# A two-layer decoder on one core: the first groups of two stages of layer 0 prepared inside the stage before, and first attention's steps reordered

## The chip, the core and the metric

The kernel runs on one core of a Trainium2 chip. The metric is the device time of one execution in microseconds (us). The kernel before was run three times: 3530.05 us median, 3529.0 to 3537.34. A core has five engines that work side by side, each with its own queue of instructions: PE (matrix multiplication and transposes, with weight loads as a second track), DVE (vector), ACT (activation), POOL (GpSimd), and SP, which here issues DMAs. An engine works off its queue in order; it waits where an operand, or the memory for its result, isn't ready.

## The reference

The input x is [32, 100, 256] in fp32: 32 sequences of 100 positions. The context is [32, 361, 192]. Cut to what matters here:

```
x = x + attention(layernorm(x))                 # layer 0: causal, 16 heads of 16
x = x + cross_attention(ctx, layernorm(x))      # keys and values from layernorm(ctx) and from
                                                # layernorm(x); q and k rms-normed; 4 heads of 64
x = x + dense_layer(layernorm(x))               # see below
# layer 1: attention, cross attention, routed experts, likewise added to x

def cross_attention(ctx, latents):
    xn, ln = layernorm(ctx) * g + b, layernorm(latents) * g + b
    q  = ln @ Wq.T
    kv = concat([xn @ Wkv.T, ln @ Wlkv.T])      # 361 + 100 keys
    ...

def dense_layer(x):
    q_in = rope(x)                              # queries and keys from rope(x), values from x
    a  = causal_attention(q_in @ Wq.T + bq, q_in @ Wk.T + bk, x @ Wv.T + bv)
    x1 = layernorm(x + a @ Wo.T + bo)
    gates = softmax(x1 @ Wg.T + bg)             # the best 2 of 8 experts, by their gates
    return layernorm(x1 + sum(gate_e * (x1 @ We_e.T + be_e)))
```

## The kernel before

**Stages.** Layer 0 has three: first attention (from about 8 to 290 us of the profile), cross attention (290 to 774) and the dense layer, attention with rope followed by the experts (774 to 1300). Layer 1 follows with three stages that the change leaves alone. x stays on the chip, as eight tiles `xs[g]`, one for each group of G = 4 sequences (NG = 8 groups, B = 32 sequences).

**What sets the order.** Each stage's body stands in an `in_order()` block: PE, DVE, ACT and POOL get their instructions in the order in which the code calls them. DMAs on SP are placed by a scheduler. PSUM is shared by all stages: two double tiles for scores (`sc_tile`) and four banks for everything else (`mm_tile`), handed out in rotation as they come free.

**Both attentions of layer 0** are made by one function, `heads_attention` (L275). `norm(g, part)` makes the normed rows of a group in four parts; `turn(g)` returns them transposed; `queries_or_keys(g, m)` makes one of four pieces of the group's queries and keys. Its loop (from L461) has one step for each sequence s. With i = s % 4, a step issues, in this order: the scores of s+1 (L356) and their mask's first half; for i = 0 the transposes of the next group, for i = 1 piece 1, for i = 2 pieces 2 and 3; for i = 1 and 3 a part of the next norm; division of the sums of s-1 (`divided`: four transposes L418, reciprocal L423, product L425); `lowered` (maximum on DVE, L376, subtraction on POOL, L377) of the first half and the second mask; `turn_weights(s)` (16 transposes L389, copies of eT on ACT, L394); for i = 0 piece 0; for i = 2 `norm(g + 1, 1)`; then the second `lowered`, the values, the transposes of o (L431), the exponentials (L382) and the output. A caller's `fill(s, part)` is called at four places of a step. First attention calls it with an empty `fill`. There `norm` does two things: part 1 is the statistics (four BATCH_NORM_STATS2, four aggregates and two small operations), part 2 the centring (L183). Its transposed rows are copied out of PSUM one half by DVE (L131) and one by ACT (L133).

**Cross attention** starts with a prologue: contexts 0 and 1 loaded, both of context 0's parts of the norm, the latent statistics and centring of group 0 (`latents`, parts 0, 1 and 2), the first part of context 1's, and the transposed latents. Its loop runs from n = -4 to B, and each step works on several sequences at once: contexts are loaded six ahead, normed five ahead, transposed four ahead, keys and values made three ahead. The latents' own keys, values and queries (`own_keys_values`, tile x_wl in the profile's names) come in each step behind the output of the sequence before. `keys_turned` transposes keys and queries and copies them to kT (ACT, L724) and qT (DVE, L732), two buffers each.

**The dense layer** has its `norm` at L934: part 0 the statistics, part 1 the scaled rows xl (four activations on ACT, L192), part 2 eight transposes (L949) with two copies to xlT on ACT (L952), part 3 the rope on DVE (L960 to L965: xrT). In `heads_attention` all four parts run for group 0 before the first scores, and for group 1 after the first exponentials. The expert weights (f0_we, 2 MB) and their bias are loaded at the end of first attention, with the stage's other weights; the first matmul that reads them stands at 887.5 us.

Of the kernel before, what the change touches and what calls it, by code (L numbers as in the profile page):

```python
# [18 lines left out]
P = 128  # L19
B, T, D = 32, 100, 256  # L20
S2, DC = 361, 192
G = 4
# [4 lines left out]
E = 8  # L27
# [39 lines left out]
def kernel(ctx: ExitStack, tc: tile.TileContext, io: dict, out: bass.AP):  # L67
# [207 lines left out]
    def heads_attention(pool, w, wo, bias, norm, turn, res, fill):  # L275
# [171 lines left out]
        with in_order():  # L447
            for part in range(4):
                norm(0, part)
# [9 lines left out]
            for part in range(4):  # L459
                norm(1, part)  # L460
            for s in range(B + 1 + fill.steps):  # L461
                g, i = s // G + 1, s % G
                more = s + 1 < B
                if more:
                    ps = scores(s + 1)
                    masked(s + 1, 0, ps[0])
                if g < NG:
                    if i == 0:
                        turned_[g] = turn(g)
                    for m in ((), (1,), (2, 3), ())[i]:  # L470
                        queries_or_keys(g, m)
                if i in (1, 3) and g + 1 < NG:
                    norm(g + 1, i - 1)
                fill(s, 0)
                if 1 <= s <= B:
                    divided(s - 1)
                if more:
                    lowered(s + 1, 0)
                    masked(s + 1, 1, ps[1])
                if s < B:  # L480
                    turn_weights(s)
                fill(s, 1)
                if i == 0 and g < NG:
                    queries_or_keys(g, 0)
                if i == 2 and g + 1 < NG:
                    norm(g + 1, 1)
                if more:
                    lowered(s + 1, 1)
                    values(s + 1)
                if 1 <= s <= B:  # L490
                    turn_sums(s - 1)
                if more:
                    exponentials(s + 1, 0)
                if s < B:
                    sums(s)
                fill(s, 2)
                if 1 <= s <= B:
                    output(s - 1)
                if more:
                    exponentials(s + 1, 1)  # L500
                if i == 3 and g + 1 < NG:
                    norm(g + 1, 3)
                fill(s, 3)
# [11 lines left out]
    x0_wo = weight(w1, "x0_wo", D, D)  # L515
    with tc.tile_pool(name="a0", bufs=2) as pool:
# [19 lines left out]
        def fill(s, part):  # L536
            pass
# [11 lines left out]
    f0_we = weight(w2, "f0_we", D, E * D)  # L549
    f0_eb = plain(w2, "f0_eb", [E, D])  # L550
    rope = plain(w2, "rope", [P, 3, T])
    kch = CCH + [(S2, T)]
    NK = S2 + T
    with tc.tile_pool(name="x0", bufs=2) as pool, tc.tile_pool(name="x0p", bufs=1) as fixed:


        cbuf, kbuf, mbuf = [], [], []
        for n in range(2):
            cb = fixed.tile([P, 3, DC], F32, tag=f"cb{n}", name=f"cb{n}")
            nc.gpsimd.memset(cb[96:128, 2, :], 0.0)  # L560
            cbuf.append(cb)
            mb = fixed.tile([T, NK], F32, tag=f"mb{n}", name=f"mb{n}")
            nc.gpsimd.memset(mb[:, S2:], 0.0)
            mbuf.append(mb)
# [9 lines left out]
        def latents(g, part):  # L574
            if part < 2:
                lns[g] = stats(xs[g], G, twice=True, tag="l", half=part, got=lns.get(g))
            else:
                ln = pool.tile([T, G, D], F32, tag="ln", name="ln", bufs=1)
                centered(ln, xs[g], G, lns[g])
                lns[g] = ln  # L580

        def latents_turned(ln):
            lnT = pool.tile([P, 2, GT], F32, tag="lnT", name="lnT")
            transposed(lnT, ln, "x0_lg", "x0_lb", tiles=mm_tile)
            return lnT

        cbs, cns, cTs, kbs, kns, vbs, kTs, exs, eTs, oTs = {}, {}, {}, {}, {}, {}, {}, {}, {}, {}

        def context(b):
            cb = cbuf[b % 2]  # L590
            nc.sync.dma_start(
                cb[:, 0:2, :], io["ctx"][b, 0:256].rearrange("(c p) d -> p c d", p=P)
            )
            nc.sync.dma_start(cb[:105, 2, :], io["ctx"][b, 256:S2])
            cbs[b] = cb

        def context_normed(b, part):
            if part == 0:
                cns[b] = stats(cbs[b], 3, P, tag="c")
            else:  # L600
                cn = pool.tile([P, 3, DC], F32, tag="cn", name="cn")
                centered(cn, cbs.pop(b), 3, cns[b], P)
                cns[b] = cn

        def context_turned(b, c):

            if c == 0:
                cTs[b] = pool.tile([P, 2, S2], F32, tag="cT", name="cT")
            cn, cT = cns[b], cTs[b]
            pt = mm_tile()  # L610
            for k, (k0, kn) in enumerate(CCH):
                if c == 0:
                    nc.tensor.transpose(pt[:, k0 : k0 + kn], cn[:kn, k, 0:P], ident[:kn, :kn])
                    continue
                for e in range(2):
                    nc.tensor.matmul(
                        pt[64 * e : 64 * e + 64, k0 : k0 + kn], cn[:kn, k, P:DC],
                        ident[:kn, :kn], start=True, stop=True, tile_position=(0, 64 * e),
                    )
            gain, bias = col("x0_xg", c), col("x0_xb", c)  # L620
            if c == 0:
                return lambda: nc.scalar.activation(
                    cT[:, 0, :], pt[:, :S2], AF.Identity, bias=bias, scale=gain
                )
            cns.pop(b)
            return lambda: nc.vector.tensor_scalar(
                cT[:, 1, :], pt[:, :S2], gain, bias, ALU.mult, ALU.add
            )
# [54 lines left out]
        def squares(b):  # L683
            sq = pool.tile([P, 5, D], F32, tag="sq", name="sq", bufs=1)
# [26 lines left out]
        def keys_turned(b, c):  # L711
            if c == 0:
                kTs[b] = [
                    pool.tile([P, 2, NK], F32, tag="kT", name="kT"),
                    pool.tile([P, 2, T], F32, tag="qT", name="qT"),
# [121 lines left out]
        lns, lnTs = {}, {}  # L837

# [4 lines left out]
        with in_order():  # L843
            for b in range(2):
                context(b)
            context_normed(0, 0)
            latents(0, 0)
            context_normed(0, 1)
            latents(0, 1)
            latents(0, 2)  # L850
            context_normed(1, 0)
            lnTs[0] = latents_turned(lns.pop(0))


            for n in range(-4, B + 1):
# [6 lines left out]
                at(n - 1, output)  # L862
                at(n + 2, roots)
# [26 lines left out]
                at(n + 1, divided, 0)  # L890

# [37 lines left out]
    with tc.tile_pool(name="f0", bufs=2) as pool:  # L929
        xls = {}  # L930

        xrTs, xlTs = {}, {}

        def norm(g, part):  # L934


            if part == 0:
                xls[g] = stats(xs[g], G, tag="n", shift=True)
            elif part == 1:
                xl = pool.tile([T, G, D], F32, tag="xl", name="xl", bufs=3)  # L940
                scaled(xl, xs[g], G, xls[g])
                xls[g] = xl
            elif part == 2:
                xl2 = xls[g].rearrange("p g (d two) -> p g d two", two=2)
                xlT = xlTs[g] = pool.tile([P, 2, GT], F32, tag="xlT", name="xlT")
                for c in range(2):
                    ps = mm_tile()
                    for i in range(G):
                        nc.tensor.transpose(  # L949
                            ps[:, i * T : (i + 1) * T], xl2[:, i, :, c], ident[:T, :T]  # L950
                        )
                    nc.scalar.copy(xlT[:, c, :], ps[:, :GT])  # L952
            if part == 3:
                xlT = xlTs[g]
                xrT = xrTs[g] = pool.tile([P, 2, GT], F32, tag="xrT", name="xrT")
                xwT = pool.tile([P, 2, GT], F32, tag="xwT", name="xwT", bufs=1)
                l4, r4, w4 = (
                    x.rearrange("p c (i t) -> p c i t", t=T) for x in (xlT, xrT, xwT)
                )
                nc.vector.tensor_tensor(r4, l4, bc(bc(rope[:, 0], 1, G), 1, 2), ALU.mult)  # L960
                for c in range(2):
                    nc.vector.tensor_tensor(
                        w4[:, c], l4[:, 1 - c], bc(rope[:, 1 + c], 1, G), ALU.mult
                    )
                nc.vector.tensor_tensor(xrT, xrT, xwT, ALU.add)  # L965
# [98 lines left out]
        def gated(n):  # L1064
            if n < E * NG:

                tag = "xg" if n < 2 * (B - 2 * G) else ("xg", "xlT", "xrT")[(n // 2 + 1) % 3]
                xg = pool.tile([P, 2, GT], F32, tag=tag, name="xg")
# [83 lines left out]
        def gates():  # L1152
# [7 lines left out]
            pool, f0_w, f0_wo, ("f0_bq", "f0_bk", "f0_bv"), norm, turn_group, res, fill  # L1160
        )

# [1149 lines left out]
```

## Time and profile before

One execution was profiled. It took 3532.22 us; its span from the first to the last instruction is 3530.5 us. The mean granted clock of PE was 0.977 of full speed.

| stretch, us | length | PE busy | DVE busy | ACT busy | POOL busy | granted clock |
|---|---|---|---|---|---|---|
| start, 0 to 8 | 8 | 0.00 | 0.23 | 1.28 | 1.03 | 1.00 |
| first attention, 8 to 290 | 282 | 254.62 | 197.96 | 162.36 | 112.48 | 0.95 |
| cross attention, 290 to 774 | 484 | 466.80 | 338.91 | 289.11 | 366.58 | 0.98 |
| dense layer, 774 to 1300 | 526 | 479.19 | 365.84 | 231.56 | 208.18 | 0.97 |
| layer 1, 1300 to the end | 2230.5 | 2146.92 | 966.24 | 919.20 | 555.17 | 0.98 |

A line of a timeline has the start, the busy time of the group, the engine, the line of the code, the operation, the tiles written and read by their names in the program, the shapes, the count, and in square brackets the idle time before it with the instruction that ended it. A wait in brackets on PE is time in which PE did nothing. The granted clock is a mean over the stretch that is asked for.

### The profile page before, as it was taken

The page shows a single profiled execution, that of the slowest core. Times are in us where ns is not written, and L with a number is a line of the kernel's source. Part 1 is how long each engine was busy: PE and PEld are TensorE (multiplying, and loading weights), DVE is VectorE, ACT ScalarE, POOL GpSimd, SP SyncE. Part 2 cuts the span into 40 slices and gives each one's busy share as a digit, 9 for nine tenths or more (in the row PEclk, how much of TensorE's full clock was granted, in tenths as well). Part 3 has the DMA queues.
Part 4 walks back from the last instruction along what each step waited for, and adds up shares of the span by engine and source line. Part 5 has one row for each costly group of instructions (what it writes and reads, how often), then busy time and mean ns, then how long its engine had stood idle before and what let it go on. Part 6 is the DMA issues. An engine that isn't in the chain of part 4 may idle for free. (4 is left out here: it accounts for less than half of the span.)

```text
span 3530.5 us, 66384 instructions
## 1 busy us (share of the span) xinstructions
PE 3347.5 (95%) x25978; PEld 2258.8 (64%) x25978; DVE 1869.2 (53%) x5328; ACT 1603.5 (45%) x3533; POOL 1243.4 (35%) x917
## 2 busy tenths in 40 slices
PE   7998999988999978999899999999999989999997
PEld 5675666656666643333566666666666658899997
DVE  5777777747777646655455465564645542011111
ACT  4664666656544315567454454544444442211111
POOL 3445887854434330001223333333333332012221
PEclk9999999999999989999999999999999999999999
DMA  2001100000111111000100000000000003456665
GB/s 84 2 2 61 26 23 23 20 18 9 29 29 27 36 47 26 1 1 1 46 10 19 21 24 20 26 21 19 24 23 19 24 24 109 143 168 192 181 181 146
DMA packets 109218, 168.15 MB, mean 48 GB/s; under 512 B 14996, under 2 KB 89628, under 8 KB 108444
## 3 DMA queue, kind: packets, MB, share of 16 engines
q1 hardware_dynamic: 94238, 145.60, 13.7%
q0 software_dynamic: 12688, 15.36, 2.4%
q8 instruction: 207, 3.39, 0.4%
q10 hardware_dynamic: 1982, 2.95, 0.2%
q14 instruction: 103, 0.84, 0.1%
HBM read 138.32 MB, written 28.82 MB: 47 GB/s over the span
## 5 line engine op out<-in xcount | busy, mean ns | idle before, releaser
L1704 POOL TENSOR_TENSOR ex<-ex,rc 100x1444 f32<-100x1444 f32 x128 | 332.0, 2594 | 785.2 <-DVE rc L1703 743.5
L1695 ACT ACTIVATE ex<-s,nmx 100x361 f32<-100x361 f32 x512 | 303.2, 594 | 143.6 <-DVE nmx L1686 143.6
L377 POOL TENSOR_TENSOR s<-s,nmx 100x800 f32<-100x800 f32 x128 | 195.0, 1523 | 338.9 <-DVE nmx L376 220.9
L1302 ACT ACTIVATE h<-sc,cols 128x800 f32<-128x800 f32 x256 | 222.4, 924 | 134.4 <-PE sc L1296 134.0
L1686 DVE CUSTOM_DVE_ANT_0 s<-sc,mb 100x361 f32<-100x361 f32 x512 | 250.3, 526 | 7.7 <-PE sc L1679 7.7
L2159 POOL DMA_INDIRECT acc_dram<-y,xg x57 | 89.0, 1562 | 451.1 <-DVE y L2158 242.8
L2141 ACT ACTIVATE hgT<-sc 128x1024 f32<-128x1024 f32 x57 | 58.4, 1024 | 351.2 <-PE sc L223 351.2
L223 PE MATMUL sc<-xgT,w1b 128*128 128x128 f32 x1824 | 213.1, 275 | 0.4 <-DMA w1b<-in_f_w 0.4
L2158 DVE TENSOR_SCALAR y<-mm,gx 128x256 f32<-128x256 f32 x57 | 27.6, 484 | 348.2 <-PE mm L223 348.2
L223 PEld LDWEIGHTS sc<-xgT,w1b 128*128 128x128 f32 x1824 | 208.2, 192 | 0.7 <-issue 0.6
L223 PE MATMUL mm<-wx,hgT 128*128 x912 | 206.1, 379 | 0.0
L1081 PE MATMUL mm<-xg,f_we 128*128 128x400 f32 x512 | 191.4, 517 | 14.2 <-DVE xg L1069 13.7
L1679 PE MATMUL sc<-kT,qT 64*100 64x361 f32 x1024 | 197.6, 463 | 0.0
L1651 PE MATMUL mm<-x_wa,cT 128*128 128x512 f32 (+1 forms) x512 | 191.1, 496 | 0.1
L1711 PE MATMUL mm<-ident,ex 100*128 100x100 f32 (+1 forms) x1536 | 169.0, 258 | 18.7 <-ACT kT L1633 9.7
L223 PEld LDWEIGHTS mm<-wx,hgT 128*128 128x128 f32 x912 | 169.0, 190 | 20.6
L1729 PEld LDWEIGHTS mm<-eT,vb 128*64 128x64 f32 (+1 forms) x3072 | 136.8, 137 | 67.3 <-issue 66.4
L1621 PE MATMUL mm<-cT,x_wa 128*128 128x361 f32 x512 | 178.3, 471 | 0.7 <-DVE lnT L148 0.7
L1711 PEld LDWEIGHTS mm<-ident,ex 100*128 100x128 f32 (+1 forms) x1536 | 143.6, 152 | 39.8 <-ACT kT L1633 13.9
L174 POOL TENSOR_TENSOR rs<-va,neghalf 100x4 f32<-100x4 f32 (+1 forms) x96 | 95.5, 997 | 206.2 <-DVE va L170 112.7
L1718 ACT COPY eT<-mm 128x400 f32<-128x400 f32 (+1 forms) x256 | 125.7, 491 | 90.0 <-PE mm L1711 88.5
L1729 PE MATMUL mm<-eT,vb 128*64 128x100 f32 (+1 forms) x3072 | 162.2, 254 | 0.0
(346 smaller groups left out, 7220.2 us busy)
## 6 DMA issues: line engine op xcount, KB each, us to landing
w1b<-in_f_w SPq DMA_DIRECT2D x57, 1024.0 KB
wb<-wt_dram SPq DMA_DIRECT2D x64, 200.0 KB
wx<-in_f_w SPq DMA_DIRECT2D x8, 1024.0 KB
xg<-sorted_dram SPq DMA_DIRECT2D x57, 132.5 KB
cb<-in_ctx SPq DMA_DIRECT2D x32, 192.0 KB
cT<-in_ctxT SPq DMA_DIRECT2D x32, 180.5 KB
cT<-in_ctxT SPq DMA_DIRECT2D x64, 90.2 KB
x<-in_x SPq DMA_DIRECT2D x8, 400.0 KB
```

Of the source, the lines that this page charges most:

```text
L223: nc.tensor.matmul(ps, lhsT[k], rhs[k], start=(k == 0), stop=(k == n - 1))
L377: nc.gpsimd.tensor_tensor(sm, sm, bc(nmx, 2, T), ALU.add)
L1081: nc.tensor.matmul(ps[:, :GT], f0_we[:, k, e * D + m * P : e * D + (m + 1) * P], xgs[E * g + e][:, k, :], start=(i > 0 and e == 2 * i and ...
L1302: nc.scalar.activation(h1, both[r2][:, :, :GT], AF.Tanh, bias=col("a1_b1", o))
L1621: nc.tensor.matmul(kTs[u][c][:, :S2], x1_wa[:, m * P : (m + 1) * P], cT[:, 0, :], start=True, stop=False,)
L1651: nc.tensor.matmul(ps[e][:kn, :n], cT[:, 0, at], x1_wa[:, 1024 + c0 : 1024 + c0 + n], start=True, stop=False,)
L1679: nc.tensor.matmul(ps[:T, e, :S2], qT[p0 : p0 + 64, m, tok], kT[p0 : p0 + 64, c, :], start=True, stop=True,)
L1686: nc.vector.tensor_tensor_reduce(s[:, e, :], ps[:T, e, :S2], mb, 1.0, 3.4e38, ALU.add, ALU.min, nmx[:, e : e + 1],)
L1695: nc.scalar.activation(ex[:, 2 * c + e, :], s[:, e, :], AF.Exp, bias=nmx[:, e : e + 1], scale=-1.0, accum_out=sm[:, 2 * c + e : 2 * c + e ...
L1704: nc.gpsimd.tensor_tensor(ex, ex, bc(rc, 2, S2), ALU.mult)
L1711: nc.tensor.transpose(pt[:kn, j * T : (j + 1) * T], ex[:, j, k0 : k0 + kn], ident[:T, :T])
L1729: nc.tensor.matmul(po[64 * e : 64 * e + 64, m * T : (m + 1) * T], vb[k][:kn, v0 + 64 * h : v0 + 64 * h + 64] if k < 2 else vb[2 + u % 2][: ...
```

## The change

First attention (the calls with bias None): the statistics of the next group move from behind `turn_weights` in the step with i = 2 to ahead of `divided`; the next group's rows are turned at the end of the step with i = 3, no longer after the scores of the next step; piece 0 of queries and keys moves in the step with i = 0 from behind `turn_weights` to right behind the scores.

```diff
     def heads_attention(pool, w, wo, bias, norm, turn, res, fill, ready=0):
...
-                    if i == 0:
+                    if i == 0 and g not in turned_:
                         turned_[g] = turn(g)
-                    for m in ((), (1,), (2, 3), ())[i]:
+                    for m in (((2,), (3,), (), ()) if g == 1 and ready == 2 else ((0,) if bias is None else (), (1,), (2, 3), ()))[i]:
                         queries_or_keys(g, m)
-                if i in (1, 3) and g + 1 < NG:
+                if i >= 1 and (i != 2 or bias is None) and g + 1 < NG:
                     norm(g + 1, i - 1)
...
-                if i == 0 and g < NG:
+                if i == 0 and g < NG and bias is not None and not (g == 1 and ready == 2):
                     queries_or_keys(g, 0)
-                if i == 2 and g + 1 < NG:
+                if i == 2 and bias is not None and g + 1 < NG:
                     norm(g + 1, 1)
...
                 if i == 3 and g + 1 < NG:
                     norm(g + 1, 3)
+                    if bias is None:
+                        turned_[g + 1] = turn(g + 1)
```

Cross attention: the functions of its prologue move ahead of first attention, with their tiles in a pool of their own; the prologue goes, the loop starts one step later, and first attention's `fill` does both:

```diff
         def fill(s, part):
-            pass
+            for f, *args in {
+                (B - 5, 0): ((context, 0), (context, 1)),
+                (B - 3, 0): ((context_normed, 0, 0),),
+                (B - 3, 2): ((latents, 0, 0),),
+                (B - 2, 0): ((latents, 0, 1),),
+                (B - 2, 2): ((context_normed, 0, 1),),
+                (B - 1, 0): ((context_normed, 1, 0),),
+                (B - 1, 1): ((latents, 0, 2),),
+                (B - 1, 3): ((context_normed, 1, 1),),
+            }.get((s, part), ()):
+                f(*args)
+            if s < B:
+                return
+            if part == 0:
+                lnTs[0] = latents_turned(lns.pop(0))
+            elif part < 3:
+                context_turned(0, part - 1)()
+            else:
+                latents(1, 0)
+                context(2)
+                context_normed(2, 0)
...
-            for n in range(-4, B + 1):
+            for n in range(-3, B + 1):
```

To make room, kT and qT have one buffer each instead of two, and the squares of the keys share their tile with a scratch tile of the rope. The expert weights and bias move from the end of first attention to the start of the dense layer, behind layer 1's first weights:

```diff
-    f0_we = weight(w2, "f0_we", D, E * D)
-    f0_eb = plain(w2, "f0_eb", [E, D])
...
-                    pool.tile([P, 2, NK], F32, tag="kT", name="kT"),
-                    pool.tile([P, 2, T], F32, tag="qT", name="qT"),
+                    pool.tile([P, 2, NK], F32, tag="kT", name="kT", bufs=1),
+                    pool.tile([P, 2, T], F32, tag="qT", name="qT", bufs=1),
...
+        f0_we = weight(fixed, "f0_we", D, E * D)
+        f0_eb = plain(fixed, "f0_eb", [E, D])
```

The dense layer: the body of its `norm` becomes `f0_norm(pool, tag, g, part)`, unchanged in what it computes, and is called for groups 0 and 1 in cross attention's last steps:

```diff
+                if n == B - 2:
+                    f0_norm(pool, "sq", 0, 3)
                 at(n + 2, roots)
...
                 at(n + 1, divided, 0)
+                for g_, part in {
+                    B - 8: ((0, 0),), B - 7: ((0, 1),), B - 6: ((1, 0),), B - 5: ((1, 1),),
+                    B - 3: ((0, 2),), B - 2: ((1, 2),), B: ((1, 3),),
+                }.get(n, ()):
+                    f0_norm(pool, "sq", g_, part)
```

`heads_attention` is told so by `ready = 2`: it makes no norm for groups 0 and 1. Group 1 is turned, and its pieces 0 and 1 are made, before the loop; pieces 2 and 3 follow in steps 0 and 1.

```diff
-            for part in range(4):
+            for part in range(4 if ready < 1 else 0):
                 norm(0, part)
...
-            for part in range(4):
+            if ready == 2:
+                turned_[1] = turn(1)
+                for m in range(2):
+                    queries_or_keys(1, m)
+            for part in range(4 if ready < 2 else 0):
                 norm(1, part)
```

## The prediction

> **What bounds the kernel now.** I read the page first, then busy time by stage, then the waits of TensorE (PE), then the timelines of PE, VectorE (DVE) and ScalarE (ACT) at the places that the diff touches.
>
> ```profile
> PE 3347.5 (95%) x25978; PEld 2258.8 (64%) x25978; DVE 1869.2 (53%) x5328; ACT 1603.5 (45%) x3533; POOL 1243.4 (35%) x917
> ```
>
> PE is the bound over all, so only PE's idle time and the time it runs at a lower clock can be won. The table by stage (window, length, busy us of PE, weight loads, DVE, ACT, POOL, granted clock, DMA) says where these are:
>
> ```profile
> 40.00:285.00 245.00, 229.88 (x3011) 173.06 (x3002) 179.54 (x321) 152.36 (x309) 102.59 (x130) 0.97 0.01 2
> 285.00:330.00 45.00, 35.51 (x191) 20.09 (x192) 29.45 (x97) 12.45 (x24) 16.59 (x12) 0.85 0.33 110
> 330.00:745.00 415.00, 414.12 (x3219) 275.23 (x3216) 301.67 (x948) 262.15 (x621) 331.50 (x209) 1.00 0.08 21
> 775.00:830.00 55.00, 41.05 (x413) 29.42 (x414) 30.96 (x60) 30.02 (x57) 15.53 (x20) 0.84 0.09 26
> ```
>
> First attention (40 to 285 us) leaves PE idle for 15 us, the change to cross attention (285 to 330) for 9.5 us at clock 0.85, cross attention itself for nothing, and the start of the dense layer (775 to 830) for 14 us at 0.84. The waits of PE from 40 to 285 us name one releaser (total, times, longest):
>
> ```profile
> PE mm L389 <- ACT ex L382: 12.4, 7, 2.5
> ```
>
> It happens once in each group of four sequences. One such place on PE, with the DVE rows that lead to it, and the clock after it:
>
> ```profile
> 157.76 0.85 PE L389 MATMUL mm<-ident,ex 100*100 100x100 f32 x8
> 160.57 1.29 PE L389 MATMUL mm<-ident,ex 100*100 100x100 f32 x8 [1.95 <-ACT ex L382]
> 161.65 1.92 PE L223 MATMUL mm<-a_w,xT 128*100 128x256 f32 x4
> ```
> ```profile
> 152.17 0.26 DVE L423 RECIPROCAL rc<-mm 100x16 f32<-100x16 f32 x1 [2.26 <-PE mm L418]
> 154.60 0.42 DVE L161 BATCH_NORM_STATS2 st<-x 100x6 f32<-100x256 f32 x1
> 156.93 0.98 DVE L376 TENSOR_REDUCE nmx<-s 100x8 f32<-100x800 f32 x1
> ```
> ```profile
> 162.00:164.00 2.00, 2.00 (x11) 1.22 (x13) 1.97 (x3) 0.84 (x3) 1.52 (x1) 0.50 0.03 8
> ```
>
> The next group's statistics (154.60 to 156.93, 2.33 us) push back the row maximum, so the subtraction on POOL, so the exponential. PE waits 1.95 us and then runs some 3.4 us at half clock (1.92 us for value matmuls that take 1.03 elsewhere). Just before, DVE idles for 2.26 us.
>
> The two changes of stage:
>
> ```profile
> 289.15 1.11 PE L223 MATMUL mm<-a_wo,oT 128*100 128x256 f32 x4 [0.47 <-ACT oT L437]
> 294.56 1.98 PE L210 MATMUL mm<-ident,ln 100*128 100x100 f32 x8 [4.30 <-DVE ln L183]
> 298.47 4.01 PE L223 MATMUL mm<-x_wl,lnT 128*100 128x512 f32 x8
> ```
> ```profile
> 781.08 7.86 PE L223 MATMUL mm<-xrT,f_w 128*128 128x400 f32 x16 [3.60 <-DVE xrT L965]
> 799.06 2.58 PE L949 MATMUL mm<-ident,xl 100*128 100x100 f32 x8 [8.37 <-ACT xl L192]
> 809.12 0.96 PE L356 MATMUL sc<-kT,qT 32*100 32x100 f32 x32
> ```
>
> PE waits 4.30 us for the first normed rows of cross attention, 3.60 us for the rope of group 0 and 8.37 us for the normed rows of group 1 of the dense layer. No arithmetic goes away in this change: what can be won is these gaps and the half clock behind them.
>
> **Part A, first attention's order.** In the third step of a group the statistics move ahead of the reciprocal: they start when the first mask addition ends (149.9) and end at 152.2, inside the 2.26 us idle; reciprocal and o are at most 0.1 us late. The row maximum then starts at 154.7 instead of 156.93, POOL's 1.52 us and ACT's 0.87 us follow, and the exponential ends about 158.2, not 160.5. In the fourth step the second half of the transposes then follows the first without a wait, at full clock. Late next is DVE: x addition, mask (0.98), the centring of the next group's rows (1.76 for four), reciprocal and o end at 160.8. So the o transposes run at 161.0, sums and output to 163.1; the next scores could start at 163.05 instead of 165.92, 2.9 us sooner. Part of this is given back: the eight row transposes (0.91, only moved) stand ahead of these scores, and the q matmuls now stand ahead of the weight transposes and wait for ACT's copy of the turned rows, behind an exponential that is only 0.9 us earlier (end 165.9, copy to 166.4). This is an **added wait** of 0.8 to 1.25 us; behind it on PE stand the transposes of back and of the weights, and ACT's copies wait for those. The scores after come at about 172.0 instead of 173.95: 2.0 us a group. Six groups: **12 us**. Ends: 2 (each new wait brings the half clock, as five of the six old ones did; the group without it is 1.7 us shorter than these) and 18 (the 2.9 is kept).
>
> [...] The row says 0.50 after a gap of 1.95 us. I go by the rows: none for the waits of 0.8 to 1.25 (gaps of 1.05 and 1.29 us elsewhere show no drop), 2 us for the one of 2.5 us in part C. [...]
>
> **Part B, first attention into cross attention.** Context statistics (1.6 us), latent statistics (two of 1.1), centring (0.96 twice, 1.38) and the transposes go into the last four steps of first attention. Steps without a norm there take 5.91 us on PE and have DVE idle 2 to 3 us each; what doesn't fit delays o and back: I count 0.5, 1.3 and 1.2 us in three steps, 3.0 together. Against that, from the last output's end (290.26) to the first latent matmul (298.47), 8.2 us, little stays: lnT at once, its copies, transposes of the context. With the 3.0 included it starts at 294.8, 3.7 sooner; it takes 2.74 as in the steady loop, not 4.01 (1.3); and the 0.5 us of waits in the first context's products go: **5.5 us**. The keys' wait on POOL (2.84 us at 319.91) stays. Ends: 0 (steps delayed twice as much, gaps still at half clock) and 9. On SP's queue contexts 0 and 1 load at step 27, contexts 2 and 3 ahead of the dense layer's weights; that hides the 2.73 us wait for a context at 302.73. The 2 MB of expert weights go to the start of the dense layer, behind layer 1's weights: they took part in the 10 us at 308 GB/s after 290; first use is at 887.5, over 90 us later. Nothing; if the cover were gone, some 7 us.
>
> **Part C, cross attention into the dense layer.** Cross attention's loop has no slack on PE: each of four steps that carry statistics (2.33 on DVE) or scaling (2.07 on ACT) delays the copies of qT or kT that free the banks for the latent matmuls, by about 0.8 us: 3.3 us lost. Transposes, copies and rope of group 0 fall in the waits of the tail (2.60 and 1.29 us at 755 and 759): nothing. From the last output's end (774.35) I count: rope of group 1 on DVE to +3.4, the query bias to +3.75, now behind the rope; PE's four q and k products of 1.34 us to +5.4; ACT's copies to +7.45; scores(0) at +6.9 (before +15.4). Then two q products of group 1, scores(1) at +10.95 (before +27.2). Masks, maxima and exponentials of step 0 end at +14.5 (they took 6.4 us); the copies of group 1's q stand behind these on ACT and hold the banks, so PE waits some 2.5 us, weights to +17.6, and scores(2) comes at +19.75, before at +34.77: 15.0. By scores(4) it is 16.8, as the half clock of 795 to 806 has gone. Less 2 for a new drop, less 3.3: **11.5 us**, ends 5 and 17. One buffer for kT and qT costs nothing: ACT writes kT at 705.6, the scores that read the one before end at 701.3.
>
> **Sum.** 12 + 5.5 + 11.5 = 29 us. Span 3530.5 becomes 3501.5; the profiled execution took 3532.2, 1.7 more; the median of the runs is 3530.05, 2.2 below that. 3501 to 3503: I take 3502.
>
> **Rivals.**
> 1. *The new waits take one part back.* In A the new wait on ACT brings the half clock (A 2 instead of 12), or in C the banks hold PE 8 us longer. For it: five of six gaps. Against it: the new gap is shorter. Time 3512 to 3516.
> 2. *Both.* 29 - 10 - 8, and B at half: about 3523, no change by measure.
> 3. *Slower: one buffer for kT.* If ACT's kT copy had to wait for the scores of the sequence before, each of 31 steps of 14.08 us grows. With 1.5 us a step, 46 - 29: 3548. It decides from 40/31 = 1.3 us a step, which needs scores that end 5.6 us later against the copy than now. Against it: the 4.3 us of slack, and an unchanged order of PE in these steps. A shift of the shared PSUM banks would cost the same way; by the order of instructions 6 of the 64 latent matmul groups wait for ACT after, 3 before, so at most 3 us.
>
> **Chances.** A difference under 0.3% (10.6 us) can't be told from none. Forecast 0.60, rival 1 0.20, rival 2 0.11, rival 3 0.09: faster 0.80, same 0.11, slower 0.09. All parts at their best, 44 us, give 3486; some room below makes 3482; at the top rival 2 is taken in: 3528.
>
> **What would show it.** A: the wait of L389's transposes on the exponential falls from 12.4 to under 3 us, a group from 33.56 to about 31.6, and a new wait on the xT copy appears. B: the gap of 4.30 is gone, last steps a little longer. C: scores(2) about 20 us after the last output, 8.37 gone. Wrong if cross attention's steps exceed 14.08, or if a clock of 0.50 follows the new waits in first attention.

## The result, and the profile after

The changed kernel takes 3512.05 us (median of six runs, 3508.92 to 3513.11), the kernel before on the same chip 3530.19. The ratio is 0.9944, 95% interval 0.9931 to 0.9957: faster by 15 to 24 us, where 29 were forecast. The profiled execution took 3510.88 us, with a span of 3508.4, against 3532.22 and 3530.5 before: 22.1 us by the trace. In the kernel after, line numbers from about 275 on are one or more higher (L389 is L390, L382 is L383).

The waits of PE from 40 to 280 us in the kernel after (total, times, longest):

```profile
PE mm L223 <- ACT xT L133: 5.9, 6, 1.0
PE mm L390 <- DVE qT L312: 3.3, 13, 0.6
PE mm L419 <- ACT back L411: 2.2, 2, 1.5
PE mm L390 <- ACT ex L383: 0.5, 2, 0.3
```

The 12.4 us of waiting for the exponential are down to 0.5. In its place stands, once in each of six groups, the wait for ACT's copy of the turned rows, 1.0 us each. One of them on PE:

```profile
161.91 0.94 PE L223 MATMUL mm<-xT,a_w 128*128 128x400 f32 x2
163.83 0.94 PE L223 MATMUL mm<-xT,a_w 128*128 128x400 f32 x2 [0.98 <-ACT xT L133]
```

Two of the four matmuls of piece 0 run at once, the other two 0.98 us late; the granted clock stays at 1.00. The end of first attention, on PE and, ahead of the second wait, on DVE:

```profile
276.90 0.64 PE L419 MATMUL mm<-ident,back 128*100 128x128 f32 x4 [1.52 <-ACT back L411]
280.70 0.36 PE L432 MATMUL mm<-ident,o 100*128 100x100 f32 x2 [1.23 <-DVE o L426]
288.59 2.74 PE L223 MATMUL mm<-x_wl,lnT 128*100 128x512 f32 x8
```
```profile
275.73 2.27 DVE L183 TENSOR_SCALAR cn<-cb,mv,rs 128x192 f32<-128x192 f32 x3
279.85 0.25 DVE L424 RECIPROCAL rc<-mm 100x16 f32<-100x16 f32 x1
```

The 4.30 us gap is gone and the first latent matmul follows the last output at once (288.59). But the last steps now hold waits of 1.52 us for back and 1.23 us for o; before, the longest of these were 0.53 and 0.90 us. A context's centring and, from 278.25, another context's statistics stand on DVE ahead of the reciprocal that o needs. In cross attention, a step that carries a group's statistics, on PE and on DVE:

```profile
679.81 2.82 PE L223 MATMUL mm<-x_wl,lnT 128*100 128x512 f32 x8 [0.74 <-ACT kT L799]
683.27 1.45 PE L872 MATMUL mm<-ident,ex 100*128 100x100 f32 x14 [0.47 <-POOL ex L863]
```
```profile
680.09 0.16 DVE L173 TENSOR_SCALAR sh<-mv 100x4 f32<-100x4 f32 x1
680.16 0.16 DVE L862 RECIPROCAL rc<-sm 100x2 f32<-100x2 f32 x1
680.24 0.40 DVE L807 TENSOR_SCALAR qT<-mm,gains 128x200 f32<-128x200 f32 x1
```

The second reciprocal and the copy of qT stand behind the statistics. In the steps before it the latent matmuls take the bank that the copy of qT frees, 0.21 us before they start; here they take one that ACT's copy of kT frees, and wait 0.74 us. That copy is not late itself (it starts 14.08 us after the one before); the wait comes from the other bank. Then PE waits 0.47 us for POOL, whose second multiplication needs that reciprocal. The dense layer's start:

```profile
765.83 5.54 PE L223 MATMUL mm<-xrT,f_w 128*128 128x400 f32 x16
781.82 0.55 PE L390 MATMUL mm<-ident,ex 100*100 100x100 f32 x4 [1.84 <-ACT qT L306]
787.24 0.96 PE L357 MATMUL sc<-kT,qT 32*100 32x100 f32 x32
```

The first q products run right behind cross attention's last output, and the waits of 3.60 and 8.37 us are gone; PE waits 1.84 us, and then 0.60, for banks that ACT holds.

The next table goes by the starts of the score matmuls in the timelines (us, profiled executions). "Six groups" is the time from the scores of sequence 4 to those of sequence 28; the next column goes from there to cross attention's first scores. Its first 25 steps take 355.2 to 355.3 us in every kernel and are left out; its last six follow, and then the time to the scores of the dense layer's third sequence, here called the third scores.

| kernel | first scores | six groups of first attention | from there to cross attention's first scores ("the stretch") | last six steps of cross attention | to the third scores of the dense layer | span |
|---|---|---|---|---|---|---|
| before | 22.47 | 201.36 | 72.23 | 75.54 | 48.08 | 3530.5 |
| after | 23.83 | 191.60 | 68.11 | 80.13 | 33.90 | 3508.4 |
| after, again | 24.19 | 191.58 | 68.95 | 80.14 | 34.34 | 3509.1 |
| undo_a | 24.50 | 200.85 | 67.15 | 80.16 | 35.31 | 3520.2 |
| stats_only | 24.23 | 186.03 | 68.62 | 80.14 | 35.45 | 3505.7 |
| xt_dve | 23.89 | 184.12 | 68.95 | 80.10 | 33.86 | 3501.2 |
| undo_b | 23.52 | 195.00 | 62.87 | 80.13 | 35.48 | 3508.1 |
| late_b | 23.06 | 195.09 | 62.73 | 80.13 | 35.17 | 3507.2 |
| we_only | 23.22 | 201.52 | 70.63 | 75.54 | 46.54 | 3528.7 |
| undo_c | 24.28 | 191.57 | 67.11 | 80.73 | 45.05 | 3523.0 |
| so_pq | 24.55 | 186.00 | 67.11 | 75.55 | 30.07 | 3493.0 |
| so_pq_ub | 24.10 | 190.95 | 62.91 | 76.31 | 29.74 | 3495.6 |
| so_pq_hb | 23.22 | 186.06 | 63.56 | 76.45 | 29.76 | 3491.0 |
| best3 | 22.33 | 186.04 | 62.13 | 75.56 | 32.00 | 3490.4 |

### The profile page after: what moved, and what is told of

Its sections match the earlier page's. It is cut to its first block, busy times and chain, and to the rows that moved or that the text cites. A ratio compares the mean times of both kernels' runs of the same rounds, so it can differ in the third digit from the quotient of the medians.

```text
span 3508.4 us, 66389 instructions
## 1 busy us (share of the span) xinstructions
PE 3339.7 (95%) x25978; PEld 2249.4 (64%) x25978; DVE 1872.9 (53%) x5328; ACT 1601.2 (46%) x3533; POOL 1245.6 (36%) x917
```

## The experiments

Times are medians; each has its ratio to the kernel before on the same chip, with its 95% interval. The kernel after has 0.9944 (0.9931 to 0.9957). Most single steps below are smaller than these intervals, so they are read from the traces. Chips differ: before took 3530.19 us on the first and 3532.84 to 3534.94 with the experiments.

**undo_a: first attention's old order, the rest as after.**

```diff
-                if i >= 1 and (i != 2 or bias is None) and g + 1 < NG:
+                if i in (1, 3) and g + 1 < NG:
                     norm(g + 1, i - 1)
...
-                if i == 2 and bias is not None and g + 1 < NG:
+                if i == 2 and g + 1 < NG:
                     norm(g + 1, 1)
...
-                    if bias is None:
-                        turned_[g + 1] = turn(g + 1)
```

(and piece 0 of queries and keys back behind `turn_weights`)

> First attention's order as before, the rest as after. Theory 1 (the old wait on the exponential and the half clock behind it were the cost, part A worth 9.8 us in the trace): six groups back at 33.6 us, the wait of L390 on L383 back at some 12 us, time about 3522. Theory 2 (the half clock falls by chance, so A is worth only the order): at most 2 us slower than after, 3512 to 3514.

3520.24 us, ratio 0.9958 (0.9941 to 0.9975). The six groups are back at 200.85 us and the wait is there again:

```profile
PE mm L390 <- ACT ex L383: 11.7, 6, 2.0
```

Theory 1 holds for the size. What the groups are made of says more. In the kernel before they take 33.75, 33.75, 32.17, 33.68, 33.79 and 34.22 us; in undo_a 33.73, 32.18, 33.69, 33.78, 33.74 and 33.73. One in six is 1.6 us shorter, the third there, the second here. In the kernel before, the wait in that short group is as long as in the others:

```profile
128.39 0.93 PE L389 MATMUL mm<-ident,ex 100*100 100x100 f32 x8 [1.95 <-ACT ex L382]
```

The clock behind it stays at 1.00, and behind the same wait 32 us later it is 0.50. The two differ in where the wait falls. In the traces of before and after, all changes of the granted clock lie 3.413 us or a whole multiple of it apart (50 and 40 stretches of one clock, to within 0.01 us; the half clock behind the second wait lasts from 160.94 to 164.36); the pieces of this length, counted on from there, are called clock windows here. These are the window in which the short group's wait ends, the one behind it, and the one that holds the next group's wait:

```profile
126.81:130.22 3.41, 1.83 (x14) 1.53 (x14) 3.38 (x9) 2.45 (x5) 0.72 (x3) 1.00 0.00 0
130.22:133.63 3.41, 3.41 (x77) 2.59 (x76) 2.56 (x4) 1.85 (x4) 2.94 (x2) 1.00 0.02 5
157.53:160.94 3.41, 1.46 (x16) 1.22 (x14) 3.41 (x8) 1.30 (x3) 2.17 (x4) 1.00 0.00 0
```

The number behind the length is PE's busy time, the last but two is the clock. An edge of the grid, at 126.81, cuts the first wait (126.44 to 128.39), so 1.58 us of idle time are left in its window, and the next window runs at full clock. The second wait lies whole in its window, which leaves 1.95 us, and the next one, from 160.94, runs at half. Of the six such waits in before, the other five leave 1.95 to 2.45 us in one window, and a clock of 0.50 follows each. A group of 33.75 us is 0.38 us shorter than ten windows, so the wait shifts against the grid from group to group: the first three begin 0.41 and 0.01 us behind an edge and 0.37 us ahead of one. By this, which group keeps its clock is a matter of phase.

So the half clock costs some 1.6 us and falls in five groups of six. Against the group without it (32.18), a group of after (31.93) wins only 0.25 us. Most of what part A won is the clock.

**stats_only: of first attention's order, only the statistics move.**

```diff
-                    for m in (((2,), (3,), (), ()) if g == 1 and ready == 2 else ((0,) if bias is None else (), (1,), (2, 3), ()))[i]:
+                    for m in (((2,), (3,), (), ()) if g == 1 and ready == 2 else ((), (1,), (2, 3), ()))[i]:
...
-                    if bias is None:
-                        turned_[g + 1] = turn(g + 1)
```

> Of first attention's order only the statistics are moved; rows are turned and piece 0 of queries is made where they were before. Theory 1 (statistics alone take the wait away; the turning a step sooner only adds the 0.98 us wait on the xT copy and 0.8 us to the step with i = 0): groups of about 31.1 us, some 5 us faster than after, 3507. Theory 2 (the turn has to move as well, or its transposes and piece 0 hold the next step): groups of 32 us or more, 3512 or slower.

3506.73 us, 0.9918 (0.9901 to 0.9935). Groups of 31.0 us, 5.6 less for six than after: theory 1, by the trace; the intervals of the times touch. As it came with the change, turning a step sooner costs 0.94 us a group.

**xt_dve: both halves of the turned rows are copied by DVE.**

```diff
-            transposed(xT, xns.pop(g), tiles=mm_tile)
+            for c in range(2):
+                nc.vector.tensor_copy(xT[:, c, :], ps[c][:, :GT])
```

(from group 2 on, behind the same eight transposes)

> After, but from group 2 on DVE copies both halves of first attention's turned rows out of PSUM, so that no copy stands behind the second exponential on ACT. Theory 1 (the 0.94 us that the turn costs a group is the added wait of piece 0 on ACT's copy): the wait of 0.98 us goes, groups of 31.0 us as with the statistics alone, 5 to 6 us below after. Theory 2 (it is the place of the transposes and of piece 0, ahead of the weights): groups of 31.7 us or more, within 2 us of after.

3504.67 us, 0.9924 (0.9908 to 0.9941). Groups of 30.69 us, and of PE's waits from 40 to 245 us one kind is left:

```profile
PE mm L390 <- DVE qT L312: 3.3, 13, 0.5
```

So theory 1 holds: the cost was the copy on ACT behind the exponential. With the copy on DVE the earlier turn wins 0.3 us a group over stats_only; with it on ACT it loses 0.94.

**undo_b: the prologue back in cross attention's loop.**

```diff
         def fill(s, part):
-            for f, *args in {
...
+            pass
...
+            context_normed(0, 0)
+            latents(0, 0)
...
-            for n in range(-3, B + 1):
+            for n in range(-4, B + 1):
```

> Cross attention's prologue again behind first attention, loop from n = -4, the rest as after. Theory 1 (part B is worth what the trace shows between the last steady step of first attention and the first steady scores, 4.1 to 4.8 us): about 3516.5. Theory 2 (what B wins is lost again in the cross attention it feeds, as its loop is bound elsewhere): within 1 us of after. The start of the kernel tells a third thing: if the first scores are again at 22.5 us instead of 23.8, the early pool has to do with the later start.

3507.5 us, 0.9922 (0.9905 to 0.9938): not slower than after, against theory 1. The span is level with after (3508.1 against 3508.4), as theory 2 had it, but not for its reason: cross attention loses nothing. The trace shows why. The prologue did not go back behind first attention; its instructions stand in the middle of it. DVE and PE in undo_b:

```profile
211.34 0.34 DVE L161 BATCH_NORM_STATS2 st<-cb 128x6 f32<-128x192 f32 x1
...
223.53 0.32 DVE L183 TENSOR_SCALAR ln<-x,mv,rs 100x256 f32<-100x256 f32 x1
223.77 0.42 DVE L426 TENSOR_TENSOR o<-mm,rc 100x256 f32<-100x256 f32 x1
```
```profile
224.33 0.36 PE L432 MATMUL mm<-ident,o 100*128 100x100 f32 x2 [1.93 <-DVE o L426]
```

Context statistics stand there from 211 us on, the context's centring from 217.84 to 219.97, and a piece of the latents' centring right ahead of o, which PE then waits for. The sixth group takes 35.16 us instead of 31.93, but the stretch falls from 68.11 to 62.87 us. Two blocks that are each in a fixed order are still merged by the scheduler. The first scores (23.52 us, after 23.83) do not move with the prologue; the early pool is in this kernel too.

**late_b: as undo_b, and the early tiles are opened behind first attention too.**

```diff
-    ctx_cm = tc.tile_pool(name="x0e", bufs=2, side="right")
...
     close_weights(0)
...
+    ctx_cm = tc.tile_pool(name="x0e", bufs=2, side="right")
```

> After, but with cross attention's prologue and its tiles opened behind first attention as before. Theory 1 (most of B comes from the moved expert weights): that stretch takes 68 to 69 us, as in after (68.1), time within 1 us of after. Theory 2 (B comes from the early prologue): 72 us, 4 us slower than after.

3510.74 us, 0.9934 (0.9917 to 0.995), stretch 62.73, sixth group 35.24: as undo_b, and as neither theory had it. The prologue is merged into first attention wherever the code puts it. In the kernel before, with its tiles in cross attention's pools, it ran at 290 us. That memory of its own is what frees it is an inference; no run changed that alone (the later load of the expert weights, in we_only, does not free it).

**we_only: the kernel before, with the expert weights loaded late.**

```diff
-    f0_we = weight(w2, "f0_we", D, E * D)
-    f0_eb = plain(w2, "f0_eb", [E, D])
...
+        f0_we = weight(fixed, "f0_we", D, E * D)
+        f0_eb = plain(fixed, "f0_eb", [E, D])
```

> The kernel before with one edit: the expert weights and their bias are loaded at the start of the dense layer. Theory 1 (their 2 MB crowded out the contexts at 290 to 300 us, so that moving them is part of what the change wins there): the 2.7 us wait for a context is gone, the stretch from the last steady step of first attention to the first steady scores of cross attention falls from 72.2 us to 68 or 69, time 3 to 4 us below before. Theory 2 (the load was hidden but for a wait that something else takes over, as the prediction had it): within 1 us of before.

3531.05 us, 0.9994 (0.9984 to 1.0003). The stretch falls by 1.6 us, to 70.63, and no wait for a context is left, but PE's wait for the first latent rows (4.30 us before) is the same:

```profile
295.76 1.97 PE L210 MATMUL mm<-ident,ln 100*128 100x100 f32 x8 [4.31 <-DVE ln L183]
```

Both theories miss: the wait of 2.7 us goes, and 1.6 us of it show in the stretch, an amount that the timing alone can't tell from nothing.

**undo_c: the dense layer makes its first norms itself.**

```diff
-                if n == B - 2:
-                    f0_norm(pool, "sq", 0, 3)
...
-                }.get(n, ()):
-                    f0_norm(pool, "sq", g_, part)
...
-            pool, f0_w, f0_wo, ("f0_bq", "f0_bk", "f0_bv"), norm, turn_group, res, fill, 2
+            pool, f0_w, f0_wo, ("f0_bq", "f0_bk", "f0_bv"), norm, turn_group, res, fill
```

> The dense layer makes its own first norms again, the rest as after. Theory 1 (part C is worth 11.1 us by the trace, net of 4.6 lost in cross attention's last steps): about 3523, cross attention's steps at 14.08 to the end, and 14 to 16 us lost between its last output and the third scores. Theory 2 (C is given back later in the dense layer, which waits for something with a fixed date): 3512 to 3516.

3524.3 us, 0.997 (0.9959 to 0.9982), 14.6 us more span than after. Theory 1 for the time; but cross attention's steps are not all back at 14.08. One takes 19.27 us, as group 0's scaling is merged there on ACT, between the copies of keys:

```profile
690.18 1.09 ACT L192 ACTIVATE xl<-x,sh,rs 100x256 f32<-100x256 f32 x2 [2.91 <-POOL sh L176]
691.18 0.35 ACT L734 COPY kb<-mm 105x256 f32<-105x256 f32 x1
691.43 1.09 ACT L192 ACTIVATE xl<-x,sh,rs 100x256 f32<-100x256 f32 x2
```

So this kernel does not quite undo part C either: early norms in a place that nobody chose cost 5.2 us, those of the change 4.6.

**so_pq: three waits taken out.** In first attention only the statistics move (as in stats_only). In cross attention, statistics and scaling of the dense layer's first groups move to steps in which DVE and ACT idle. In the dense layer, the first exponentials move behind the copies of group 1's queries:

```diff
-                    B - 8: ((0, 0),), B - 7: ((0, 1),), B - 6: ((1, 0),), B - 5: ((1, 1),),
                     B - 3: ((0, 2),), B - 2: ((1, 2),), B: ((1, 3),),
...
+                for g_, part in {
+                    B - 6: ((0, 0),), B - 5: ((1, 0), (0, 1)), B - 4: ((1, 1),),
+                }.get(n, ()):
+                    f0_norm(pool, "sq", g_, part)
                 at(n + 2, keys_normed)
...
                 lowered(0, hf)
-                exponentials(0, hf)
+                if ready < 2:
+                    exponentials(0, hf)
...
                     queries_or_keys(1, m)
+                for hf in range(2):
+                    exponentials(0, hf)
```

> After with three edits: in first attention only the statistics move; statistics and scaling of the dense layer's first groups stand ahead of keys_normed in cross attention (steps 26 to 28), where DVE and ACT idle; the exponentials of step 0 of the dense layer stand behind the copies of group 1's first queries on ACT. Theory 1 (new waits in all three places are what the change gave back): first attention 5.6 us, cross attention's steps at 14.08 to the end (4.5 us), third scores of the dense layer 2 to 4 us sooner: 12 to 14 us below after. Theory 2 (the waits only move on to POOL and ACT): 6 us below after, from first attention alone.

3499.14 us, 0.9903 (0.9887 to 0.992), clear of after. Theory 1 in all three places: six groups in 186.0 us, cross attention's last six steps 75.55, as in the kernel before (75.54), and the third scores 3.8 us sooner. In cross attention DVE's statistics now end in a gap that was there:

```profile
705.38 0.18 DVE L173 TENSOR_SCALAR sh<-mv 100x4 f32<-100x4 f32 x1
706.55 0.18 DVE L778 TENSOR_SCALAR rn<-rt 128x20 f32<-128x20 f32 x1 [1.00 <-POOL rt L771]
```

Behind them DVE still waits 1.00 us for POOL. On PE in the dense layer the 1.84 us wait for banks is a wait of 0.34 for the exponential:

```profile
768.97 1.03 PE L390 MATMUL mm<-ident,ex 100*100 100x100 f32 x8 [0.34 <-ACT ex L383]
```

**so_pq_ub: so_pq with the prologue as in undo_b.**

> As so_pq, and cross attention's prologue is left to the scheduler, with the early tiles (as in undo_b). Theory 1 (by hand in the last steps it costs first attention's end 6.6 us, by the scheduler in the middle 3.4): 2 us below so_pq. Theory 2 (without the turn's wait the middle of first attention has no room on DVE either): equal to so_pq or slower.

3497.52 us, 0.9896 (0.988 to 0.9913), within the interval of so_pq. By the trace the groups take 4.95 us more and the stretch 4.2 less: theory 2.

**so_pq_hb: so_pq with the prologue's pieces in DVE's gaps.**

```diff
-                (B - 3, 0): ((context_normed, 0, 0),),
...
+                (4, 0): ((context, 0), (context, 1)),
+                (8, 1): ((context_normed, 0, 0),),
+                (12, 1): ((context_normed, 0, 1),),
+                (16, 1): ((context_normed, 1, 0),),
+                (20, 1): ((latents, 0, 0),),
+                (24, 1): ((latents, 0, 1),),
+                (26, 0): ((context_normed, 1, 1), (latents, 0, 2)),
```

> As so_pq, but cross attention's prologue is spread by hand over first attention: its pieces in steps 8, 12, 16, 20, 24 (behind turn_weights, where DVE idles for 1.5 us) and 26 (the place of the statistics, which the last group has no need of). Theory 1 (the prologue costs where DVE has no idle time, not by being early): groups stay at 31.0, the last steps at 5.9, tail at some 62 us instead of 67.1: 5 us below so_pq, 0.989 of before. Theory 2 (the tail is long for the half clock and the keys' wait on POOL, whoever makes the norms): tail of 65 us or more, within 2 us of so_pq.

3493.47 us, 0.9893 (0.9876 to 0.9909), which the timing can't tell from so_pq. Groups stay at 31.0 us and the stretch falls from 67.11 to 63.56: theory 1, with 3.5 of its 5 us.

**best3: so_pq_hb with the key buffers cleared early.**

```diff
+    for n in range(3):
+        kb = early_ctx.tile([P, 5, D], F32, tag=f"kb{n}", name=f"kb{n}", bufs=1)
+        nc.gpsimd.memset(kb[96:128, 2:5, :], 0.0)
+        kbuf.append(kb)
...
-        for n in range(3):
-            kb = fixed.tile([P, 5, D], F32, tag=f"kb{n}", name=f"kb{n}")
-            nc.gpsimd.memset(kb[96:128, 2:5, :], 0.0)
-            kbuf.append(kb)
```

> As so_pq_hb, and the clearing of the key buffers (three memsets on POOL, 2.4 us) is ahead of the first statistics, with the buffers in the early pool. Theory 1 (DVE's first centring takes 2.94 us instead of 1.9 because these memsets run beside it): centring of 1.4 us, first scores 1.0 to 1.5 us sooner, at 22.5 us, and about 1.3 us below so_pq_hb. Theory 2 (the first centring is slow for the arrival of data): 2.9 us again, equal to so_pq_hb.

3492.58 us, 0.989 (0.9874 to 0.9907): 0.9 us below so_pq_hb, which the timing can't tell apart. Its first scores stand at 22.33 us instead of 23.22. The first centring on DVE, in the kernel after and in best3:

```profile
11.84 2.94 DVE L183 TENSOR_SCALAR xn<-x,mv,rs 100x256 f32<-100x256 f32 x4 [1.24 <-POOL rs L174]
```
```profile
11.12 1.43 DVE L183 TENSOR_SCALAR xn<-x,mv,rs 100x256 f32<-100x256 f32 x4 [1.24 <-POOL rs L174]
```

Theory 1: 2.94 us beside POOL's memsets of the key buffers, 1.43 without. Its last column in the table is 2.2 us longer than that of so_pq_hb; a half clock from 745.20 to 752.03, which so_pq_hb does not have there, goes with that. This is the lowest median, 40 us below before. The copy of xt_dve was not tried together with it.

**after_again: the changed kernel once more.**

> The changed kernel once more, unedited, beside the others on the same chip. All theories: 0.993 to 0.996 of before; groups of 31.9 us, cross attention's tail steps 4.6 us long, as in the first profile.

3511.6 us, 0.9945 (0.9928 to 0.9961), as expected. Its table row shows what repeats to a tenth of a us (groups, cross attention) and what varies by 0.4 to 0.8 (the changes of stage). The clock has a part in that. PE's waits of 1.84 and 0.60 us at the start of the dense layer are in both executions of this one kernel. In the first they lie in one clock window; in the second an edge, at 784.31, cuts the longer one:

```profile
780.10:783.51 3.41, 1.09 (x9) 0.75 (x10) 1.81 (x2) 3.41 (x7) 2.94 (x2) 1.00 0.83 348
```
```profile
780.90:784.31 3.41, 2.26 (x24) 1.31 (x16) 3.34 (x5) 2.26 (x4) 2.62 (x3) 1.00 0.95 327
784.31:787.73 3.42, 2.13 (x15) 1.63 (x16) 0.81 (x1) 3.42 (x9) 2.11 (x4) 1.00 0.68 287
```

The idle time in a window is 2.32 us in the first execution, and the clock is 0.50 in the next window; in the second it is 1.15 and 1.29 us, and the clock stays at 1.00. The third scores stand 21.3 us behind the last output in the first, 19.7 in the second.

## Why the prediction was right, and where it was short

The direction and the places were right: L389's wait went from 12.4 to 0.5 us, the wait on the xT copy came, the third scores stand 21.3 us behind the last output (19.75 forecast), and the time lies in the range. The size was short: 29 us were forecast and 22.1 show in the trace. The time, 3512 us, is even the low end of what rival 1 gave (3512 to 3516), but not by rival 1's mechanism: no half clock came behind the new waits of first attention, and the banks of the dense layer did not cost 8 us more. By the prediction's own steps:

- **Part A: 12 forecast, 9.8 measured** (201.36 to 191.60). The added wait was named and its length was right (0.8 to 1.25; 0.98). Mis-sized was the gain per group: 2.0 in each of six groups, while one of the six old groups had no half clock to lose; there the change won 0.25. The row that the prediction went by, 0.50 behind a gap of 1.95 us, holds for the old order: in before, 0.50 follows five of the six gaps of 1.95 to 2.45 us. Had the old groups lost no clock at all, A would have been about 1.5 us (an estimate: six times the 0.25 of that one group). The prediction's low end, the half clock behind the new waits, did not come: it is 1.00 there.
- **The start: 0 forecast, 1.4 lost**, and 0.2 more in the first group. The prediction had no term for what the moved pool does at the beginning. The memsets of the key buffers on POOL began 0.9 us behind the start of DVE's first centring and now begin 0.4 us behind it; the centring went from 1.90 to 2.94 us, and best3, which clears these buffers earlier, has 1.43. The rest is a first centring that starts 0.35 us later, which differs as much between kernels with the same start.
- **Part B: 5.5 forecast, 4.1 measured.** Mis-sized was the delay of the last steps, 3.0 us. Counted from the same score matmul, the last output ended 32.2 us later in the kernel before and ends 38.9 us later now, 6.7 more; 2.9 of these are the transposes of the latents and of the first context, which PE did behind the last output before. So the first latent matmul starts 1.6 us sooner (0.8 in the second execution), not 3.7. The steps' DVE had two or three us of idle time in all, but not ahead of the reciprocal. The later load of the expert weights, costed at nothing, took 1.6 us off the stretch in we_only; how much of part B it is in the kernel after was not run, and the stretch of after differs by 0.8 us between two executions.
- **Part C: 11.5 forecast, 11.6 measured** to the third scores and the two behind them (9.6 and 2.0). That this is so close is luck, as two errors cancel: the steps that carry norms lost 4.6 us, not 3.3, as a step with statistics costs 1.67 us and not 0.8; a wait for a bank was right, and POOL's multiplication behind the second reciprocal was missed. The start of the dense layer won 1.4 more than forecast. The half clock that was deducted there did come, but after_again shows that it need not.
- **Later: 0 forecast, 1.8 lost**, 0.6 up to the dense layer's last score matmuls and 1.3 behind them. No run was made for it; it stays open. The 1.3 stands, at 1.0 to 2.4 us, in every kernel made from after, and not in we_only (0.2).
- **Profile and median.** The profiled execution of before lies 2.0 us above its median, that of after 1.2 below, so the medians differ by less than the traces: by 18 us, and by 21 with after_again.
- **The rivals.** One buffer for kT costs nothing: cross attention's first 25 steps take 355.26 us, 355.18 before (14.08 us each, every fourth 14.77). The banks of rival 1 did hold PE in the dense layer, for 1.84 and 0.60 us with a half clock behind, not for 8 more.

## What to carry to other kernels

Preparing a stage's first work inside the stage before pays where PE waited (here some 14 us at the third scores), but each piece has to go where its engine idles, ahead of nothing that PE needs next: the same norms cost cross attention 4.6 us or nothing, and the same prologue made the end of first attention 3.5 us longer or not, by place alone. A wait is worth more than its length where a lower clock follows it (in before some 1.6 us behind waits of 1.95), and that can differ from one execution to the next (after and after_again, at the start of the dense layer). Look at what else is queued on the engine that a moved step's copy lands on: a copy of 0.5 us behind an exponential cost more than the earlier start won. And a block written "in order" stays in order in itself only: the scheduler merged the prologue into the block ahead (undo_b, late_b), probably because its tiles had memory of their own.

## What the runs showed of the hardware

In the traces of before and after all changes of the granted clock lie whole multiples of 3.413 us apart, and a wait of the same length has either clock behind it: in before, of two waits of 1.95 us, the one that leaves 1.58 us of idle time in its window (126.81 to 130.22) is followed by 1.00, the one that leaves 1.95 (157.53 to 160.94) by 0.50. These two traces have 1943 windows at full clock from 40 to 3480 us (the ends of matmuls are modelled). The 41 that half clock follows have 1.19 to 3.41 us of idle time, the 1902 that full clock follows at most 1.78; between 1.19 and 1.78 both occur.

DVE's first centring takes 2.94 us beside POOL's memsets of the key buffers (after, so_pq_hb) and 1.43 without these (best3). In the first attention of before the same four instructions take 1.76 to 1.77 us where they overlap the end of POOL's subtraction and two short memsets (five groups), and 1.37 to 1.38 where POOL is idle (two).
